# Second layer of a two-layer graph network: one tile in every fourth block by TensorE products instead of a gather

## The chip, the cores and the metric

The kernel runs on one core of one Trainium2 chip. Its measure is the device time of one execution in microseconds (us). The engines are PE (TensorE: matmuls; PEld is its weight load), DVE (VectorE), ACT (ScalarE), POOL (GpSimd) and SP (SyncE). Each works through its own instructions in order, and they meet at semaphores. Here POOL issues only gathers in the main part, and SP issues plain DMAs.

## The reference, cut to what matters

There are 6250 nodes with 128 features and 200,000 edges (src, dst), sorted by dst. Two layers follow each other, each on a normalized x: a graph attention layer, then a tensor product layer. What the change touches is the second one:

```python
h = relu(layernorm(x))
s, v = h[:, :32] @ W_up_s / sqrt(32), einsum(h[:, 32:], W_up_v) / sqrt(32)
w0, w1, w2, w3 = split(silu(silu(edge_feats @ A1 + b1) @ A2 + b2) @ A3, 4)   # per edge
ss, vs = s[src], v[src]                                                     # the gather
m = [ss * y_s * w0, (vs . y_v) / sqrt(3) * w3, ss * y_v * w1, vs * y_s * w2]  # 256 per edge
message = segment_sum(m, dst) / 10
x = x + [message_s @ W_out_s, message_v @ W_out_v] / 8
```

Because the edges are sorted by dst, the sum over an edge's target is a matmul with a one-hot matrix of local target numbers.

## The kernel before, in words

An edge tile is 128 edges; a block is 16 tiles (KB), except the last with 11. There are 98 blocks (NB), 1563 tiles, and 50 node tiles (NX). The first layer leaves a table t1 in DRAM: 128 float32 values (s and v) per node. The second layer starts at L1617. It works in units of four tiles (list us), four units to a block.

The order of the work on PE, DVE, ACT and SP is the order in which the Python program calls the operations (manual_schedule with in_order). POOL holds only the gathers, also in the program's order.

For each unit i of the loop at L1795 the order is:
- at the first unit of a block: take_rows(b + 2), the gathers of the block two further on; filled, which copies a row tile into place (ACT, L1096); edge_rows(b + 2), two loads by SP (L1631, L1633); every second block a load of x (L1709).
- rows_until, which advances SP's copies of single rows (below).
- network(b + 1): one of four steps of the edge network of the next block (PE L1650 or L1654, ACT L1652 or L1657).
- tensor_weights(i + 1): the weights of the next unit (PE L1667) and their scaling by y_s (ACT L1671).
- messages(i): seven DVE operations, L1687 to L1696, which read the gathered rows z and write mj.
- one_hot(i + 1) (DVE L1101), then the end of a block (finish, L1114) and node1 (L1711), and sums1(i) (PE L1704), which adds the unit's messages into PSUM.

A gather fetches the 128 rows of one edge tile, one indirect DMA issued by POOL (L834). A block's rows land in a buffer g of the pool fz, which has five of them (L976); block 0 has z_first. A buffer is free once the block's last messages have read it.

Two ways around the gather exist. In every third block (by_row, L1057) the last tile's 128 rows are copied one by one by SP (L1082), after offsets are loaded into registers 32 at a time (L1078). rows_until (L1089) keeps this three blocks ahead, so the first unit of a layer starts with 35 steps of 4 rows. In the first layer, in the blocks of dense (L1127), tile KD = 14 is made of matmuls: the table is held in SBUF as three bf16 parts that add up to its float32 values (t0s, split at L1167), a one-hot matrix picks the rows (L1198, L1211), and since the 50 node tiles are folded into 17 steps of up to three tiles, DVE picks the right one of three results (L1217, L1219).

The first 24 tiles of the second layer are gathered early, from a copy t1z of the table in which the last three node tiles are zero. late_ends and late_rows (L1744, L1758) add the missing rows by matmuls in the first units.

PSUM has eight banks; in the second layer p_h, p_w and p_u have two each, p_n one, and held one (iota, and yp, a copy of y_v in three places by turns).

Of the kernel before, what the change touches and what calls it, by code (L numbers as in the profile page):

```python
# [965 lines left out]
def even_edges(tc, v):  # L966
# [7 lines left out]
    with ExitStack() as ctx:  # L974
# [123 lines left out]
        def one_hot(t, m, iota=iota):  # L1098

            s = s_pool.tile([P, 4, P], F32, name="s")  # L1100
# [21 lines left out]

        NR = -(-NX // 3)
        KD = KB - 2
        dense = {b for b in range(6, NB - 4) if b % 2}  # L1127


        in_order = {mybir.EngineType.PE, mybir.EngineType.DVE, mybir.EngineType.Activation,  # L1130
                    mybir.EngineType.SP}
        with tc.manual_schedule(engines=in_order), \
# [10 lines left out]
            nc.scalar.copy(iota_p, iota)  # L1143
            nc.scalar.mul(node_p, jp[:, 0:1], -1.0)


            ND = NB - 1
            key = l0d.tile([P, ND], F32, name="key")
            nc.vector.tensor_scalar(key, src_col[:, KD : ND * KB : KB], float(W0), None, op0=OP.add)
            part = l0d.tile([P, ND, 3], F32, name="part")  # L1150
            nc.vector.tensor_single_scalar(part[:, :, 1], key, float(NR * P), op=OP.is_ge)
            nc.vector.tensor_single_scalar(part[:, :, 2], key, float(2 * NR * P), op=OP.is_ge)
            nc.vector.tensor_add(part[:, :, 0], part[:, :, 1], part[:, :, 2])
            nc.vector.scalar_tensor_tensor(key, part[:, :, 0], -float(NR * P), key,
                                           op0=OP.mult, op1=OP.add)
            nc.vector.tensor_sub(part[:, :, 1], part[:, :, 1], part[:, :, 2])
            nc.vector.tensor_single_scalar(part[:, :, 0], part[:, :, 0], 0.0, op=OP.is_equal)

            order = sorted(range(NR), key=lambda k: (k > 0, 2 * NR + k < NX, k))
            half = (NR + 1) // 2  # L1160
            place = l0d.tile([P, NR], F32, name="place")
            for j, k in enumerate(order):
                nc.vector.tensor_scalar(place[:, j : j + 1], jp[:, 0:1], -1.0, float(P * k),
                                        op0=OP.mult, op1=OP.add)
            t0s = l0d.tile([P, 3, NX, ZW], BF, name="t0s")

            def split(i, n):  # L1167

                zr = l0.tile([P, 2, ZW], F32, name="zr")[:, :n]
                if i == 0:  # L1170
                    nc.vector.memset(zr[:W0, 0, :], 0.0)
                    nc.sync.dma_start(zr[W0:, 0, :], t0[: P - W0, :])
                    rest = t0[P - W0 : n * P - W0]
                    nc.sync.dma_start(zr[:, 1:], rest.rearrange("(j p) f -> p j f", p=P))
                else:
                    rest = t0[i * P - W0 : (i + n) * P - W0]
                    nc.sync.dma_start(zr, rest.rearrange("(j p) f -> p j f", p=P))
                r = l0.tile([P, 2, ZW], F32, name="zr2", bufs=1)[:, :n]
                nc.scalar.copy(t0s[:, 0, i : i + n, :], zr)
                nc.vector.tensor_sub(r, zr, t0s[:, 0, i : i + n, :])  # L1180
                nc.scalar.copy(t0s[:, 1, i : i + n, :], r)
                nc.vector.tensor_sub(t0s[:, 2, i : i + n, :], r, t0s[:, 1, i : i + n, :])

            def spread(c):

# [284 lines left out]
            for g in range(NG - 3):  # L1470
# [73 lines left out]
                if to:  # L1544
                    rows_of(n2, 6, half - 6)
                for i in range(g * 14, min(g * 14 + 14, NX), 2):
                    split(i, min(2, NX - i))
                if g == NG - 4:
                    for q in range(4):
                        ends_of(c1, q)  # L1550
# [66 lines left out]
        with tc.manual_schedule(engines=in_order), \  # L1617
                tc.tile_pool(name="l1", bufs=3) as l1, \
                tc.tile_pool(name="l1n", bufs=2) as l1n, \
                tc.tile_pool(name="l1_ps", bufs=2, space=PSUM) as l1_ps:  # L1620

            a3p = l1.tile([P, 2, P], F32, name="fa3p", bufs=1)
# [12 lines left out]
            def network(b, step):  # L1635

                c = blk[b]
                q0, second = step // 2 * 4, step % 2
                if 2 * q0 >= KT[b]:
                    return  # L1640
                if step == 0:
                    c["h2"] = []
                if step == 3 or 2 * q0 + 8 >= KT[b] and second:
                    c["yp"] = held[:, P + b % 3 * KB * 3 : P + (b % 3 + 1) * KB * 3].rearrange(
                        "p (t i) -> p t i", i=3)
                    nc.scalar.copy(c["yp"], c["yb"][:, :, 1:4])  # L1646
                p_h = l1_ps.tile([P, 4, P], F32, name="p_h")
                if not second:
                    for q in range(4):
                        nc.tensor.matmul(p_h[:, q, :], a1p[:, q0 + q, :], c["ft"], start=True, stop=True)  # L1650
                    c["h1"] = l1.tile([P, 4, P], F32, name="h1")
                    nc.scalar.activation(c["h1"], p_h, AF.Silu, bias=b1)  # L1652
                else:
                    nc.tensor.matmul(p_h.rearrange("p q e -> p (q e)"), a2p,  # L1654
                                     c["h1"].rearrange("p q e -> p (q e)"), start=True, stop=True)
# [54 lines left out]

            def node1(i, agg):  # L1711
                x_i = x_of[i][:, 0, :]
                p_n = l1_ps.tile([P, 4, P], F32, name="p_n", bufs=1)
                for q in range(2):
                    nc.tensor.transpose(p_n[:, q, :], agg[:, q * P : (q + 1) * P], ident)
                m_t = l1n.tile([P, 2, P], F32, name="m_t")
                nc.scalar.copy(m_t, p_n[:, :2])  # L1717
                for q in range(2):
                    nc.tensor.matmul(p_n[:, 2, :], m_t[:, q, :], wout[:, q, :], start=q == 0, stop=q == 1)  # L1719
                nc.vector.scalar_tensor_tensor(x_i, p_n[:, 2, :], POST, x_i, op0=OP.mult, op1=OP.add)  # L1720
                return i

            def node_out1(i):
# [34 lines left out]
            def late_rows(t):  # L1758
                if t < NE:
                    z, k0, oh = blk[t // KB]["z"], t % KB, late_ends.of.pop(t)  # L1760
                    p_n = l1_ps.tile([P, 4, P], F32, name="p_n", bufs=1)
                    for k in range(4):
                        for j in range(NL):
                            nc.tensor.matmul(p_n[:, k, :], oh[:, j, k, :], sv_late[:, j, :],
                                             start=j == 0, stop=j == NL - 1)
                    z = z[:, k0 : k0 + 4, :P]
                    nc.vector.tensor_add(z, z, p_n)

            blk = [{} for _ in range(NB)]
            us = [{"b": b, "k0": k0, "m": min(4, KT[b] - k0)}  # L1770
# [3 lines left out]
            def take_rows(b):  # L1774
                if b in early:
                    blk[b]["z"] = gather(early[b], t1, range(max(b * KB, NE), b * KB + KB), P,
                                         max(NE - b * KB, 0))
                elif b < NB:
                    blk[b]["z"] = gathered(t1, range(b * KB, b * KB + KT[b] - (b in by_row)), P)

            rows, rows_until.n, late, x_of = rows_by_row(1, t1, P), 0, [], {}
            for b in range(2):
# [5 lines left out]
            for step in range(4):  # L1788
                network(0, step)
            tensor_weights(us[0])  # L1790
            us[0]["s"] = one_hot(0, us[0]["m"], iota_p)
            ready, done = [], []
            carry = agg = None
            ends = None
            for i, u in enumerate(us):  # L1795
                b, k0, m = u["b"], u["k0"], u["m"]
                if k0 == 0:
# [11 lines left out]
                if i + 1 < NU:  # L1809
                    tensor_weights(us[i + 1])  # L1810
                late_ends(4 * (i + 2))
                messages(u)
                late_rows(4 * (i + 1))
                if i + 1 < NU:
                    n = us[i + 1]
                    n["s"] = one_hot(n["b"] * KB + n["k0"], n["m"], iota_p)
# [18 lines left out]
            p_n = l1_ps.tile([P, 4, P], F32, name="p_n", bufs=1)  # L1835
# [152 lines left out]
```

## Time and profile before

| | |
|---|---|
| Time, median of 3 runs | 3953.19 us (3948.89 to 3955.46) |
| The profiled execution's own time | 6235.86 us |
| Its span, first to last instruction | 6234.0 us |
| Mean granted PE clock in it | 0.728 |
| Busy: PE, PEld, DVE, ACT, POOL | 3133, 2416, 2621, 1191, 2872 us |
| Gathers of the main part (L834) | 2980, 945 ns each |
| Single-row copies by SP (L1082) | 7936 |
| Second layer in it, from the first gather of t1 | 3052.77 us to the end |

A line of a group shows the source line, the engine, the operation, output and inputs, how often it occurs, then busy time and mean duration in ns, then the idle time of the engine just before and what ended it. A line of the timeline shows start and duration in us, then the same names; in brackets the idle time before it and what ended that. "issue" stands for idle time in which the engine waited for nothing that the profile shows. The profiled execution is much longer than the timed ones, so times of the page and those of the runs are not compared directly.

### The profile page before, as it was taken

The page shows a single profiled execution, that of the slowest core. Times are in us where ns is not written, and L with a number is a line of the kernel's source. Part 1 is how long each engine was busy: PE and PEld are TensorE (multiplying, and loading weights), DVE is VectorE, ACT ScalarE, POOL GpSimd, SP SyncE. Part 2 cuts the span into 40 slices and gives each one's busy share as a digit, 9 for nine tenths or more (in the row PEclk, how much of TensorE's full clock was granted, in tenths as well). Part 3 has the DMA queues.
Part 4 walks back from the last instruction along what each step waited for, and adds up shares of the span by engine and source line. Part 5 has one row for each costly group of instructions (what it writes and reads, how often), then busy time and mean ns, then how long its engine had stood idle before and what let it go on. Part 6 is the DMA issues. An engine that isn't in the chain of part 4 may idle for free. (4 is left out here: it accounts for less than half of the span.)

```text
span 6234.0 us, 64789 instructions
## 1 busy us (share of the span) xinstructions
PE 3133.4 (50%) x15554; PEld 2416.2 (39%) x15554; DVE 2620.8 (42%) x6094; ACT 1190.7 (19%) x3272; POOL 2872.4 (46%) x3052
## 2 busy tenths in 40 slices
PE   2145454444444444444355555555555555555557
PEld 1133333333333333333344444444444444444445
DVE  3244444444444444444333444444443444443446
ACT  1111111111111111111122222222222222222223
POOL 6144444444454454455534444444444444444442
PEclk6567677667667766777577777777777777777778
DMA  5122222222222222222111111111111111111111
GB/s 141 41 61 58 63 59 60 61 58 58 62 60 58 58 63 59 57 61 66 54 26 39 38 39 37 39 39 39 39 36 38 39 40 39 37 37 37 40 39 26
DMA packets 230951, 311.54 MB, mean 50 GB/s; under 512 B 83328, under 2 KB 168928, under 8 KB 230560
## 3 DMA queue, kind: packets, MB, share of 16 engines
q0 software_dynamic: 96640, 204.21, 13.8%
q1 hardware_dynamic: 133632, 103.03, 5.6%
q8 instruction: 125, 2.05, 0.1%
q14 instruction: 266, 2.18, 0.1%
q10 hardware_dynamic: 288, 0.07, 0.0%
HBM read 289.79 MB, written 16.95 MB: 49 GB/s over the span
## 5 line engine op out<-in xcount | busy, mean ns | idle before, releaser
L834 POOL DMA_INDIRECT g<-ft,fsrc x2980 | 2816.1, 945 | 3241.3 <-issue 1119.4
L1704 PE MATMUL p_u<-mj,s 128*128 128x256 f32 x3126 | 930.0, 450 | 680.8 <-DVE mj L1696 572.6
L1704 PEld LDWEIGHTS p_u<-mj,s 128*128 128x128 f32 x3126 | 682.6, 226 | 865.7 <-DVE mj L1696 623.4
L1251 DVE TENSOR_TENSOR d<-er_d,p_i 128x512 bf16<-128x512 bf16 x391 | 264.5, 677 | 863.1 <-DMA er_d<-fends_d 787.6
L1101 DVE TENSOR_TENSOR s<-p_i,fdloc 128x512 f32<-128x512 f32 x782 | 533.0, 682 | 197.2 <-PE p_i L1187 135.6
L1689 DVE TENSOR_TENSOR p_w<-g,p_w 128x128 f32<-128x128 f32 x387 | 112.9, 292 | 1178.2 <-ACT p_w L1671 1024.2
L1211 PE MATMUL p_x<-t0s,fz_first 128*128 128x408 bf16 (+1 forms) x2244 | 559.6, 409 | 29.9 <-issue 29.6
L1333 PE MATMUL p_u<-g,s 128*128 128x136 f32 x3062 | 537.4, 348 | 7.2 <-issue 4.4
L1671 ACT ACTIVATE p_w<-p_w,yb 128x64 f32<-128x64 f32 x1563 | 449.7, 288 | 461.2 <-remote 238.0
L1333 PEld LDWEIGHTS p_u<-g,s 128*128 128x128 f32 x3062 | 514.8, 255 | 7.7 <-issue 7.5
L1302 PE MATMUL pe<-mx,fshift 128*128 128x1 f32 (+1 forms) x194 | 55.8, 357 | 741.9 <-issue 514.7
L1667 PE MATMUL p_w<-fa3p,h 128*128 128x256 f32 x1564 | 422.7, 395 | 0.0
L1667 PEld LDWEIGHTS p_w<-fa3p,h 128*128 128x128 f32 x1564 | 303.3, 204 | 143.5 <-issue 106.0
L1657 ACT ACTIVATE h<-p_h,fb 128x512 f32<-128x512 f32 x196 | 134.7, 687 | 1141.9 <-remote 796.3
L1211 PEld LDWEIGHTS <-fz_first 128*128 128x128 bf16 x2244 | 250.8, 115 | 244.8 <-issue 152.5
L1719 PE MATMUL p_n<-fwout,m_t 128*128 128x128 f32 x192 | 57.6, 454 | 563.6 <-ACT m_t L1717 563.6
L1302 PEld LDWEIGHTS pe<-mx,fshift 128*128 128x128 f32 (+1 forms) x194 | 47.6, 305 | 749.9 <-issue 520.1
L1654 PE MATMUL p_h<-h,fa2p 128*128 128x512 f32 x392 | 248.0, 720 | 168.5 <-ACT h L1652 145.5
L1261 PEld LDWEIGHTS <-d 128*128 128x128 bf16 x1563 | 105.9, 122 | 513.0 <-DVE d L1251 378.0
L1687 DVE TENSOR_TENSOR vy<-g,p_i 128x384 f32<-128x384 f32 x387 | 211.3, 546 | 179.6 <-ACT p_i L1646 178.1
L1652 ACT ACTIVATE h<-p_h,fb 128x512 f32<-128x512 f32 x196 | 134.3, 685 | 726.8 <-PE p_h L1650 373.8
L1719 PEld LDWEIGHTS p_n<-fwout,m_t 128*128 128x128 f32 x192 | 43.7, 316 | 576.6 <-ACT m_t L1717 576.6
(220 smaller groups left out, 3667.6 us busy)
## 6 DMA issues: line engine op xcount, KB each, us to landing
r<-ft SPq DMA_DIRECT2D x3968, 0.5 KB
r<-ft SPq DMA_DIRECT2D x3968, 0.5 KB
er_d<-fends_d SPq DMA_DIRECT2D x98, 512.0 KB
g<-ft,fsrc POOLq DMA_INDIRECT x2980
ft<-in_e_f_dram SPq DMA_DIRECT2D x98, 64.0 KB
zr<-ft SPq DMA_DIRECT2D x24, 136.0 KB
yb<-in_e_y_dram SPq DMA_DIRECT2D x98, 32.0 KB
x<-in_e_xp_dram SPq DMA_DIRECT2D x48, 64.0 KB
```

Of the source, the lines that this page charges most:

```text
L834: nc.gpsimd.indirect_dma_start(out=to[:, k, :width], out_offset=None, in_=table, in_offset=bass.IndirectOffsetOnAxis(ap=src_col[:, t : t + ...
L1101: nc.vector.tensor_tensor(s[:, :m], iota[:, None, :].to_broadcast([P, m, P]), dloc[:, t : t + m].unsqueeze(2).to_broadcast([P, m, P]), OP. ...
L1211: nc.tensor.matmul(c["p_x"][:, :m, :], c["oh", k // half][:, k % half, :], t0s[:, s, i::NR, :], start=k == 0 and s == 0, stop=k == NR - 1 ...
L1251: nc.vector.tensor_tensor(d[:, :m], ends_row.tiles[c["b"]][:, k0 : k0 + m], node_p.unsqueeze(2).to_broadcast([P, m, P]), OP.is_equal)
L1333: nc.tensor.matmul(c["p_u"][:, :ZW], c["s"][k // 4][:, k % 4, :], c["z"][:, k, :], start=c["o"] + k == 0, stop=c["o"] + k == KT[c["b"]] - 1)
L1652: nc.scalar.activation(c["h1"], p_h, AF.Silu, bias=b1)
L1654: nc.tensor.matmul(p_h.rearrange("p q e -> p (q e)"), a2p, c["h1"].rearrange("p q e -> p (q e)"), start=True, stop=True)
L1657: nc.scalar.activation(h2, p_h, AF.Silu, bias=b2)
L1667: nc.tensor.matmul(w[:, k : k + n].rearrange("p k a u -> p (k a u)"), c["h2"][q // 4][:, q % 4, :], a3p[:, :n].rearrange("p k f -> p (k f) ...
L1671: nc.scalar.activation(w[:, k, ::2, :], w[:, k, ::2, :], AF.Copy, scale=c["yb"][:, k0 + k, 0:1])
L1687: nc.vector.tensor_mul(vy, v_n, y_p)
L1704: nc.tensor.matmul(blk[b]["p_u"][:, :MW], u["s"][:, k, :], u["mj"][:, k, :], start=k0 + k == 0, stop=k0 + k == KT[b] - 1)
```

## The change

The second layer gets what the first has. In blocks 8, 12, ..., 92 (dense1, 22 of 98) tile 14 is no longer gathered. Its rows are products of a one-hot matrix with t1, held in SBUF as three bf16 parts (t1s, 38,400 bytes per partition). The table is read back from DRAM by SP in 25 pieces of two node tiles (node_tiles) and split by two ACT casts and two DVE subtractions a piece (in_three), one piece in each of the first 25 units, ahead of that unit's messages. The products of a dense block are spread over the last two units of the block before and its own first three (dense_step). node1's p_n moves into the bank of held, beside iota and yp; the bank that it leaves, p_x, serves late_rows and the new products. yp now alternates between two places, not three. The pool of s buffers in the second layer has 5, not 16. Functions for the first layer's table are shared by both (ends_in_ranges, node_tiles, in_three).

```diff
-        s_pool = ctx.enter_context(tc.tile_pool(name="fs", bufs=16))
+        s_pool = of_l0.enter_context(tc.tile_pool(name="fs", bufs=16))
...
+        dense1 = set(range(8, NB - 4, 4))
...
+        def node_tiles(pool, table, width, i, n, bufs=2):
+            zr = pool.tile([P, 2, width], F32, name="zr", bufs=bufs)[:, :n]
...
+                nc.sync.dma_start(zr, rest.rearrange("(j p) f -> p j f", p=P))
+            return zr
+
+        def in_three(pool, zr, width, t_s, i, n):
+            r = pool.tile([P, 2, width], F32, name="zr2", bufs=1)[:, :n]
+            nc.scalar.copy(t_s[:, 0, i : i + n, :], zr)
+            nc.vector.tensor_sub(r, zr, t_s[:, 0, i : i + n, :])
+            nc.scalar.copy(t_s[:, 1, i : i + n, :], r)
+            nc.vector.tensor_sub(t_s[:, 2, i : i + n, :], r, t_s[:, 1, i : i + n, :])
...
-                    c["yp"] = held[:, P + b % 3 * KB * 3 : P + (b % 3 + 1) * KB * 3].rearrange(
+                    c["yp"] = held[:, P + b % 2 * KB * 3 : P + (b % 2 + 1) * KB * 3].rearrange(
...
-                p_n = l1_ps.tile([P, 4, P], F32, name="p_n", bufs=1)
...
-            iota_p = held[:, :P]
+            iota_p, p_n = held[:, :P], held[:, 2 * P :].rearrange("p (j f) -> p j f", f=P)
...
+            key, part, place_r = ends_in_ranges(l1n)
+            t1s = l1d.tile([P, 3, NX, P], BF, name="t1s")
+
+            def dense_ends(b):
+                p_x = blk[b]["p_x"] = l1_ps.tile([P, 4, P], F32, name="p_x", bufs=1)
+                nc.tensor.matmul(p_x[:, 3, :], key[:, b : b + 1].to_broadcast([P, P]), ident,
+                                 start=True, stop=True)
+                oh = blk[b]["oh"] = l1d.tile([P, NR, P], BF, name="ohs")
+                for k, n in ((0, half), (half, NR - half)):
+                    nc.vector.tensor_tensor(
+                        oh[:, k : k + n], p_x[:, 3:4, :].to_broadcast([P, n, P]),
+                        place_r[:, k : k + n].unsqueeze(2).to_broadcast([P, n, P]), OP.is_equal)
+
+            def dense_rows(b, k0, n):
+                c = blk[b]
+                for k in range(k0, min(k0 + n, NR)):
+                    i = order[k]
+                    m = len(range(i, NX, NR))
+                    for s in range(3):
+                        nc.tensor.matmul(c["p_x"][:, :m, :], c["oh"][:, k, :], t1s[:, s, i::NR, :],
+                                         start=k == 0 and s == 0, stop=k == NR - 1 and s == 2)
...
+            def dense_step(b, q):
+                if b + 1 in dense1:
+                    if q == 1:
+                        dense_ends(b + 1)
+                    elif q > 1:
+                        dense_rows(b + 1, (q - 2) * 4, 4)
+                if b in dense1:
+                    dense_rows(b, 8 + 3 * q, 3)
+                    if q == 2:
+                        dense_taken(b)
...
+            zrs = [node_tiles(l1d, t1, P, j, 2, 3) for j in (0, 2)]
             for i, u in enumerate(us):
...
                 late_ends(4 * (i + 2))
+                if 2 * i + 4 < NX:
+                    zrs.append(node_tiles(l1d, t1, P, 2 * i + 4, min(2, NX - 2 * i - 4), 3))
+                if zrs:
+                    in_three(l1d, zrs.pop(0), P, t1s, 2 * i, min(2, NX - 2 * i))
                 messages(u)
+                dense_step(b, k0 // 4)
                 late_rows(4 * (i + 1))
```

More of the change, by code (lines that the diff above doesn't have):

```diff
@@ L1096, in filled, with one_hot @@
                 nc.scalar.copy(z[:, KB - 1, :width], rows_by_row.tiles.pop((layer, b)))
-        def one_hot(t, m, iota=iota):
-            s = s_pool.tile([P, 4, P], F32, name="s")
+        def one_hot(t, m, iota, pool=s_pool):
+            s = pool.tile([P, 4, P], F32, name="s")
             nc.vector.tensor_tensor(s[:, :m], iota[:, None, :].to_broadcast([P, m, P]),
@@ L1126, in even_edges, with ends_in_ranges @@
         KD = KB - 2
+        order = sorted(range(NR), key=lambda k: (k > 0, 2 * NR + k < NX, k))
+        half = (NR + 1) // 2
         dense = {b for b in range(6, NB - 4) if b % 2}
+        dense1 = set(range(8, NB - 4, 4))
+        def ends_in_ranges(pool):
+            ND = NB - 1
+            key = pool.tile([P, ND], F32, name="key")
+            nc.vector.tensor_scalar(key, src_col[:, KD : ND * KB : KB], float(W0), None, op0=OP.add)
+            part = pool.tile([P, ND, 3], F32, name="part")
+            nc.vector.tensor_single_scalar(part[:, :, 1], key, float(NR * P), op=OP.is_ge)
+            nc.vector.tensor_single_scalar(part[:, :, 2], key, float(2 * NR * P), op=OP.is_ge)
+            nc.vector.tensor_add(part[:, :, 0], part[:, :, 1], part[:, :, 2])
+            nc.vector.scalar_tensor_tensor(key, part[:, :, 0], -float(NR * P), key,
+                                           op0=OP.mult, op1=OP.add)
+            nc.vector.tensor_sub(part[:, :, 1], part[:, :, 1], part[:, :, 2])
+            nc.vector.tensor_single_scalar(part[:, :, 0], part[:, :, 0], 0.0, op=OP.is_equal)
+            place = pool.tile([P, NR], F32, name="place_r")
+            for j, k in enumerate(order):
+                nc.vector.tensor_scalar(place[:, j : j + 1], jp[:, 0:1], -1.0, float(P * k),
+                                        op0=OP.mult, op1=OP.add)
+            return key, part, place
@@ new lines, in node_tiles @@
+        def node_tiles(pool, table, width, i, n, bufs=2):
+            zr = pool.tile([P, 2, width], F32, name="zr", bufs=bufs)[:, :n]
+            if i == 0:
+                nc.vector.memset(zr[:W0, 0, :], 0.0)
+                nc.sync.dma_start(zr[W0:, 0, :], table[: P - W0, :])
+                rest = table[P - W0 : n * P - W0]
+                nc.sync.dma_start(zr[:, 1:], rest.rearrange("(j p) f -> p j f", p=P))
+            else:
+                rest = table[i * P - W0 : (i + n) * P - W0]
+                nc.sync.dma_start(zr, rest.rearrange("(j p) f -> p j f", p=P))
+            return zr
@@ L1144, in even_edges @@
             nc.scalar.mul(node_p, jp[:, 0:1], -1.0)
[L1147 to L1164, printed above, removed]
-            t0s = l0d.tile([P, 3, NX, ZW], BF, name="t0s")
[L1167 to L1182, printed above, removed]
+            key, part, place = ends_in_ranges(l0d)
+            t0s = l0d.tile([P, 3, NX, ZW], BF, name="t0s")
             def spread(c):
@@ L1546, in even_edges @@
                 for i in range(g * 14, min(g * 14 + 14, NX), 2):
-                    split(i, min(2, NX - i))
+                    n = min(2, NX - i)
+                    in_three(l0, node_tiles(l0, t0, ZW, i, n), ZW, t0s, i, n)
                 if g == NG - 4:
@@ L1619, in even_edges @@
                 tc.tile_pool(name="l1n", bufs=2) as l1n, \
+                tc.tile_pool(name="l1s", bufs=5) as l1s, \
+                tc.tile_pool(name="l1d", bufs=1) as l1d, \
                 tc.tile_pool(name="l1_ps", bufs=2, space=PSUM) as l1_ps:
@@ L1716, in node1 @@
                 m_t = l1n.tile([P, 2, P], F32, name="m_t")
-                nc.scalar.copy(m_t, p_n[:, :2])
+                nc.scalar.copy(m_t, p_n)
                 for q in range(2):
-                    nc.tensor.matmul(p_n[:, 2, :], m_t[:, q, :], wout[:, q, :], start=q == 0, stop=q == 1)
-                nc.vector.scalar_tensor_tensor(x_i, p_n[:, 2, :], POST, x_i, op0=OP.mult, op1=OP.add)
+                    nc.tensor.matmul(p_n[:, 0, :], m_t[:, q, :], wout[:, q, :], start=q == 0, stop=q == 1)
+                nc.vector.scalar_tensor_tensor(x_i, p_n[:, 0, :], POST, x_i, op0=OP.mult, op1=OP.add)
                 return i
@@ L1760, in late_rows @@
                     z, k0, oh = blk[t // KB]["z"], t % KB, late_ends.of.pop(t)
-                    p_n = l1_ps.tile([P, 4, P], F32, name="p_n", bufs=1)
+                    p_l = l1_ps.tile([P, 4, P], F32, name="p_x", bufs=1)
                     for k in range(4):
                         for j in range(NL):
-                            nc.tensor.matmul(p_n[:, k, :], oh[:, j, k, :], sv_late[:, j, :],
+                            nc.tensor.matmul(p_l[:, k, :], oh[:, j, k, :], sv_late[:, j, :],
@@ L1765, in late_rows @@
                                              start=j == 0, stop=j == NL - 1)
                     z = z[:, k0 : k0 + 4, :P]
-                    nc.vector.tensor_add(z, z, p_n)
+                    nc.vector.tensor_add(z, z, p_l)
+            key, part, place_r = ends_in_ranges(l1n)
[9 more added lines that the diff above has]
+                        place_r[:, k : k + n].unsqueeze(2).to_broadcast([P, n, P]), OP.is_equal)
@@ new lines, in dense_rows, with dense_taken @@
+            def dense_rows(b, k0, n):
[6 more added lines that the diff above has]
+                                         start=k == 0 and s == 0, stop=k == NR - 1 and s == 2)
+            def dense_taken(b):
+                c = blk[b]
+                z = c["z"][:, KD, :P]
+                nc.vector.tensor_scalar(z, c["p_x"][:, 0, :], part[:, b, 0:1], None, op0=OP.mult)
+                for r in (1, 2):
+                    nc.vector.scalar_tensor_tensor(z, c["p_x"][:, r, :], part[:, b, r : r + 1], z,
+                                                   op0=OP.mult, op1=OP.add)
@@ L1778, in take_rows @@
                 elif b < NB:
-                    blk[b]["z"] = gathered(t1, range(b * KB, b * KB + KT[b] - (b in by_row)), P)
+                    blk[b]["z"] = gathered(t1, [k for k in range(b * KB, b * KB + KT[b])
+                                                if not (b in by_row and k % KB == KB - 1)
+                                                and not (b in dense1 and k % KB == KD)], P)
             rows, rows_until.n, late, x_of = rows_by_row(1, t1, P), 0, [], {}
@@ L1790, in even_edges @@
             tensor_weights(us[0])
-            us[0]["s"] = one_hot(0, us[0]["m"], iota_p)
+            us[0]["s"] = one_hot(0, us[0]["m"], iota_p, l1s)
             ready, done = [], []
@@ L1815, in even_edges @@
                     n = us[i + 1]
-                    n["s"] = one_hot(n["b"] * KB + n["k0"], n["m"], iota_p)
+                    n["s"] = one_hot(n["b"] * KB + n["k0"], n["m"], iota_p, l1s)
                 if ends is not None:
@@ L1834, in even_edges @@
             first = (NX - 2) * P - W0
-            p_n = l1_ps.tile([P, 4, P], F32, name="p_n", bufs=1)
+            p_n = l1_ps.tile([P, 4, P], F32, name="p_x", bufs=1)
             for j in range(2):
```

## The prediction

> **What bounds the kernel now.** I read the page first: its span, then the rows of GpSimd (POOL), which issues the gathers.
>
> ```profile
> span 6234.0 us, 64789 instructions
> PE 3133.4 (50%) x15554; PEld 2416.2 (39%) x15554; DVE 2620.8 (42%) x6094; ACT 1190.7 (19%) x3272; POOL 2872.4 (46%) x3052
> ...
> L834 POOL DMA_INDIRECT g<-ft,fsrc x2980 | 2816.1, 945 | 3241.3 <-issue 1119.4
> ```
>
> Nothing is above 50%, and the profiled execution (6235.9 us) is 58% longer than the median of the three timed runs (3953.2 us). So the page's shares can't be taken as they stand. The timeline of the DMA queue of SP says why: first a stretch near 5533 us, then one 10 us later.
>
> ```profile
> 5533.09 6.40 SPq L1082 DMA_DIRECT2D r<-ft  x20
> ```
>
> ```profile
> 5543.74 7.07 SPq L1082 DMA_DIRECT2D r<-ft  x6
> ```
>
> A row copy costs 0.32 us in the first and 1.18 us in the second. In stretches of the second kind PE, ACT and DVE stand still as well, while POOL goes on. I take them to be the profiler's own. Outside them the kernel runs at its natural pace; all durations below are from there. Now POOL's timeline at the start of the second layer:
>
> ```profile
> 3052.77 0.94 POOL L834 DMA_INDIRECT g<-ft,fsrc  x1 [24.91 <-issue]
> 3054.01 0.95 POOL L834 DMA_INDIRECT g<-ft,fsrc  x1 [0.31 <-issue]
> ...
> 3140.14 0.94 POOL L834 DMA_INDIRECT g<-ft,fsrc  x1 [0.30 <-issue]
> 3210.88 0.94 POOL L834 DMA_INDIRECT g<-ft,fsrc  x1 [69.79 <-DVE mj L1696]
> ```
>
> Gathers start every 1.249 us. After 71 of them (8 left of block 1, 16, 15, 16, 16) POOL needs the buffer of block 1, which the last message product (L1696) of that block frees: its lead over the computation is 71 gathers, 88.7 us, and no more.
>
> Sum for the whole: first gather at 42.5 us, 2980+16+16+8 = 3020 gathers x 1.249 = 3772 us, two waits at the border of the layers (6.7 and 24.9 us): 3846 us. That leaves 107 us of the median for a wait at the start and the tail: the timed kernel fits POOL issuing gathers nearly without a break, where the profiled one can't (POOL 46% busy). Per block of the second layer POOL needs 1532/98 = 15.6 gathers, 19.5 us. The computation is faster: four units (quarters of a block) in a row start their sums (L1704) at 6083.16, 6087.40, 6090.99 and 6094.64 us, 3.8 us each, about 15.5 us a block. SP needs 42.7 rows x 0.32, 1.33 loads of offsets x 2.13 and some three copies x 0.45, 18 us.
>
> **What the Trainium skill says.** "TensorE: Matmul & The Clock Gate", section "Architectural detail: the array is 16× 32×32, not 1× 128×128", calls ACT and DVE strict FIFOs: what stands ahead in program order must be done. The trace agrees; see the 110.63 us below. The same page, section "What's actually happening", has PE's clock halved after an idle window of about 3.4 us. The trace shows half clock even after an idle 1.96 us: eight sums took 1.99 us in one unit and 3.67 us in the next. "SBUF — State Buffer", section "SBUF: two separate sides", says that DVE and GpSimd share a port pair as an exclusive lock, which a DVE operation with two SBUF inputs can hold against a GpSimd operation that reads SBUF. Here gathers took 938 to 1504 ns, median 944; the case is rare.
>
> **The change, part by part.** I set zero at the second layer's first gather from t1 (3052.77).
>
> *Gathers.* Blocks 8, 12, ..., 92 lose one each: 22 x 1.249 = 27.5 us off POOL's queue.
>
> *Products that take their place.* The first layer shows them: 51 matmuls per block, nine of 128x408 in 1.72 us, so 0.16 us each at 384 columns, 8.4 us; the two comparisons (L1198) 1.34 and 1.22 us; three operations of 0.36 us. For four blocks PE needs 4 x 15.5 + 8.4 + 0.4 = 70.8 us, DVE some 4 x 13.4 + 3.6 = 57 us, POOL (4 x 15.6 - 1) x 1.249 = 76.7 us. Both are hidden by the gathers; without that cover they would cost 8.8 us per such block on PE.
>
> *Joined banks, fewer s buffers.* node1's transposes move into the bank of iota; yp alternates between two places. The readers of the place before are a block old, and at most two s tiles live at once. Nothing, or below 1 us per two blocks.
>
> *The comparisons' constants.* 17 operations of 150 ns (L1163's row) and some eight more join DVE's queue at the border, partly between steps that t1's last rows wait for: 3 us.
>
> *The table in three parts.* This is the expensive part. In each of the first 25 units two ACT casts and two DVE subtractions stand ahead of messages(u), cast and subtraction in turn. The first layer shows such a chain, and what ACT does when the table's rows are late:
>
> ```profile
> 235.45 0.42 ACT L1179 CAST t0s<-zr 128x272 bf16<-128x272 f32 x1 [110.63 <-DMA zr<-ft]
> 235.90 0.44 DVE L1180 TENSOR_TENSOR zr<-zr,t0s 128x272 f32<-128x272 f32 x1 [66.41 <-ACT t0s L1179]
> ...
> 236.37 0.42 ACT L1181 CAST t0s<-zr 128x272 bf16<-128x272 f32 x1 [0.51 <-DVE zr L1180]
> ...
> 236.82 0.44 DVE L1182 TENSOR_TENSOR t0s<-zr,t0s 128x272 bf16<-128x272 f32 x1 [0.48 <-ACT t0s L1181]
> ```
>
> The chain takes 1.8 us. Two things make it cost more.
>
> First, SP. The table's third piece is issued in unit 0 behind that unit's rows: 35 steps of 4, 140 rows. Start of rows 2.4 us (profile) + 1.3 for the three earlier copies; 140 x 0.32 = 44.8; four more loads of offsets, 8.5; issue and landing 2.6 (236.37 to 238.59 in the first layer). It is there at 59.7 us, and unit 2 waits for it. With the chain and the messages (2.5 us) unit 2's messages end at 64 us. Before, nothing in units 2 to 7 waited for SP.
>
> Second, the loop closes. Before, messages(i) needed weights that were scaled one unit earlier, so DVE ran beside PE. Now ACT's first cast in unit i stands behind the scaling of unit i+1, that behind PE's products of unit i, those behind sums1(i-1), which wait for messages(i-1). The timeline of one unit without such casts has the pieces:
>
> ```profile
> 6058.21 0.54 DVE L1696 TENSOR_TENSOR mj<-g,p_w 128x384 f32<-128x384 f32 x1
> ...
> 6058.80 1.99 PE L1704 MATMUL p_u<-mj,s 128*128 128x256 f32 x8
> ...
> 6060.63 1.02 PE L1654 MATMUL p_h<-h,fa2p 128*128 128x512 f32 x2
> ...
> 6061.49 1.03 PE L1667 MATMUL p_w<-fa3p,h 128*128 128x256 f32 x4
> ...
> 6062.08 1.25 ACT L1671 ACTIVATE p_w<-p_w,yb 128x64 f32<-128x64 f32 x4 [2.17 <-PE p_h L1654]
> ```
>
> From the end of the messages (6058.75) to the end of the scaling (6063.33) 4.6 us, the chain 1.8, the messages 2.5: 8.9 us a unit with PE at full clock. PE idles some 5.4 us of that, so its clock will often be halved, which costs the eight sums 1.7 us: 10.6 us. I take 10.1, against 4.9 us that POOL needs for four gathers.
>
> So messages of unit 3 end at 75 us (late_ends, about 1 us, is still in the chain), of unit 23 at 75 + 20 x 10.1 = 277, of unit 24 at 287, of unit 27 at 299 (three units of 4.0, free again). POOL, once its 71 gathers are out at 89 us, waits for every block: block 10 starts at 277 (block 5's buffer), block 11 at 299 (block 6's, and block 10's gathers end at 297). Before, block 11 starts after 71 + 15 + 16 + 16 + 15 + 16 = 149 gathers, at 186 us. POOL is late by 113 us; after that it isn't stopped again. SP's queue is held back too, as each further piece waits for a buffer that the casts free, but afterwards it needs 18 us a block against POOL's 19.
>
> The sum: 113 (stall) - 21 x 1.249 (block 8's gather is saved inside the stall) + 3 = 90 us. 3953 + 90 = **4043 us**.
>
> **Bounds.** With PE always warm (8.9 us, first wait the same) unit 27 ends at 273: +64, 4017. Rows at a third less than 0.32 us, if the profiler's marks weigh on them: 15 us less, 4002. Always half clock (10.6): +101, 4054; with subtractions that delay gathers (50 x 0.44 us at most, most of them within the stall) 4075. So the likeliest case alone spans 4002 to 4075.
>
> **Rivals.**
> - *The lead covers it.* If a unit took 5.9 us or less (75 + 21 x 5.9 + 12 = 211 = 186 + 26 - 1), POOL's delay would not exceed the saving; with no delay the time is 3953 - 27.5 = 3926. For it: the lead of 71 gathers, and the engines' busy times, which alone come to under 5 us a unit. Against: ACT's and DVE's program order.
> - *Half covered.* The rows come early and the chain overlaps partly: a unit of 7 us ends at 3977.
> - *PE binds later.* If a block took PE over 17 us while it follows POOL (half clock), the products would not be hidden; at 18.5 us four blocks need 82.8 against 76.7, and 22 times 6.1 is 134 us more, about 4180. Against: the sums' spacing, and no long gaps once units follow each other every 4.9 us.
> - *The change doesn't do what it says*: 22 gathers fewer must stand in POOL's rows; nothing speaks against it.
>
> **How the numbers follow.** Likeliest 0.80; lead covers 0.09; half covered 0.06; PE binds 0.05. From 3985 to 4082 leaves out the covered case, part of the half-covered one, and PE binding. About 0.2% is what a measurement of this kernel can tell from no change. Faster 0.10, same 0.02, slower 0.88.
>
> **What would show it.** In the changed profile: POOL's 71 gathers, then a wait for message products before each of blocks 6 to 11; ACT waiting for zr some 60 us (more where the profiler slows SP); in units 3 to 24 the casts behind the scaling and the sums a full loop apart, about 9 to 11 us; 2958 gathers in L834's first row; later PE no busier than POOL. I am wrong if messages in those units come every 5 to 6 us outside the slowed stretches, or if POOL isn't stopped there.

## The result, and the profile after

The changed kernel takes 4083.03 us (median of 4 runs, 4080.18 to 4085.91), the kernel before 3951.32 us (median of 4, 3948.89 to 3955.46): a ratio of 1.0331, 95% interval 1.0318 to 1.0344. It is 132 us slower, where the prediction said 90 us, and lies just above the predicted range. One thing has to be known of the times below: on three of the chips every kernel, the one before too, took about 1.6 times as long, because in stretches PE, DVE, ACT and SP stand still there; each run is compared with the kernel before on its own chip, and sizes are read from chips without such stretches.

The page of the changed kernel has its span (its own time is 4082.87 us, so this execution is like the timed ones), busy times and gathers:

```profile
span 4081.1 us, 67346 instructions
PE 2950.3 (72%) x16720; PEld 2298.7 (56%) x16720; DVE 2722.3 (67%) x6279; ACT 1233.1 (30%) x3322; POOL 2862.2 (70%) x3030
...
L834 POOL DMA_INDIRECT g<-ft,fsrc x2958 | 2805.8, 949 | 1162.6 <-issue 910.2
```

2958 gathers instead of 2980: the change does what it says. Each takes 0.95 us, but in this profile they start 1.252 us apart (median), so a POOL without a break shows as 76% busy, no more. In the page's 40 slices it is so in nearly all of the second layer, and at 20% just after the middle. POOL's timeline at that place, the start of the second layer, first its 71st and 72nd gather, then the first of block 10:

```profile
2139.56 0.95 POOL L834 DMA_INDIRECT g<-ft,fsrc  x1 [0.30 <-issue]
2175.30 0.94 POOL L834 DMA_INDIRECT g<-ft,fsrc  x1 [34.79 <-DVE mj L1708]
```

```profile
2363.11 0.94 POOL L834 DMA_INDIRECT g<-ft,fsrc  x1 [28.07 <-DVE mj L1708]
```

After 71 gathers, counted from the layer's first one (2051.45 us), POOL waits 35, 29, 26, 29, 28 and 7 us, once before each of blocks 6 to 11. The trace puts four of these waits down to message products (L1708, which was L1696), the third to nothing that it shows and the last to ACT; but each ends 0.3 to 0.8 us after the last message product of the block whose buffer is needed. To see what they cost, take the start of the 230th gather after the layer's first, less 230 x 1.25 us: it is late by 155 us. There is one more wait, of 1.9 us, before the 179th gather; from the 180th on none is over 0.32 us. So nearly all of the loss comes from the first 25 units, in which the table is built. One of these units, from the end of its predecessor's messages to its own, in the timeline:

```profile
2210.03 0.55 DVE L1708 TENSOR_TENSOR mj<-g,p_w 128x384 f32<-128x384 f32 x1
...
2210.64 3.78 PE L1716 MATMUL p_u<-mj,s 128*128 128x256 f32 x8 [5.51 <-DVE mj L1708]
...
2214.21 1.91 PE L1666 MATMUL p_h<-h,fa2p 128*128 128x512 f32 x2
...
2215.92 1.45 PE L1679 MATMUL p_w<-fa3p,h 128*128 128x256 f32 x4
...
2217.41 1.26 ACT L1683 ACTIVATE p_w<-p_w,yb 128x64 f32<-128x64 f32 x4 [0.56 <-PE p_w L1679]
2218.59 0.40 ACT L1168 CAST t1s<-zr 128x256 bf16<-128x256 f32 x1
2219.02 0.43 DVE L1169 TENSOR_TENSOR zr<-zr,t1s 128x256 f32<-128x256 f32 x1 [7.83 <-ACT t1s L1168]
...
2219.92 0.42 DVE L1171 TENSOR_TENSOR t1s<-zr,t1s 128x256 bf16<-128x256 f32 x1 [0.47 <-ACT t1s L1170]
...
2222.28 0.55 DVE L1708 TENSOR_TENSOR mj<-g,p_w 128x384 f32<-128x384 f32 x1
```

Read it downwards: sums, network step, weights, scaling, cast, subtraction, messages, one behind the other, and then the sums of the next unit. That is the predicted loop, and it takes 12.25 us here. The products on PE are all slower than in the unit that the prediction shows: from the first sum to the start of the scaling it is 6.8 us, where it was 3.3 us there. Units 3 to 24 come 11.62 us apart on average (prediction: 10.1).

### The profile page after: what moved, and what is told of

It is laid out like the page before. It is cut to its first block, busy times and chain, and to the rows that moved or that the text cites. A ratio compares the mean times of both kernels' runs of the same rounds, so it can differ in the third digit from the quotient of the medians.

```text
span 4081.1 us, 67346 instructions
## 1 busy us (share of the span) xinstructions
PE 2950.3 (72%) x16720; PEld 2298.7 (56%) x16720; DVE 2722.3 (67%) x6279; ACT 1233.1 (30%) x3322; POOL 2862.2 (70%) x3030
## 5 line engine op out<-in xcount | busy, mean ns | idle before, releaser
L1716 PE MATMUL p_u<-mj,s 128*128 128x256 f32 x3126 | 805.9, 403 | 228.9 <-DVE mj L1708 227.8
L1716 PEld LDWEIGHTS p_u<-mj,s 128*128 128x128 f32 x3126 | 603.4, 200 | 374.2 <-DVE mj L1708 291.5
L1342 PE MATMUL p_u<-g,s 128*128 128x136 f32 x3062 | 492.7, 329 | 0.4 <-DVE g L1337 0.4
L1220 PE MATMUL p_x<-t0s,fz_first 128*128 128x408 bf16 (+1 forms) x2244 | 474.0, 365 | 0.0
L1342 PEld LDWEIGHTS p_u<-g,s 128*128 128x128 f32 x3062 | 470.7, 236 | 0.5 <-DVE g L1337 0.4
L1337 DVE TENSOR_TENSOR g<-g,pe 128x1024 f32<-128x1024 f32 x193 | 234.6, 1216 | 4.9 <-ACT g L1328 4.7
L1703 DVE TENSOR_REDUCE vd<-vy 128x128 f32<-128x384 f32 x391 | 230.0, 588 | 0.0
L1662 PEld LDWEIGHTS p_h<-ft,fa1p 128*128 128x128 f32 x1568 | 211.8, 196 | 17.2 <-issue 4.2
L1662 PE MATMUL p_h<-ft,fa1p 128*128 128x128 f32 x1568 | 212.0, 279 | 4.2 <-DMA ft<-in_e_f_dram 4.2
L1704 DVE TENSOR_TENSOR mj<-p_w,yb 128x384 f32<-128x384 f32 x391 | 214.9, 550 | 0.0
```

The costliest lines, as they stand in the source:

```text
L1220: nc.tensor.matmul(c["p_x"][:, :m, :], c["oh", k // half][:, k % half, :], t0s[:, s, i::NR, :], start=k == 0 and s == 0, stop=k == NR - 1 ...
L1337: nc.vector.tensor_mul(zh, zh, p_a[:, k0 : k0 + m].unsqueeze(3).to_broadcast([P, m, H, D]))
L1342: nc.tensor.matmul(c["p_u"][:, :ZW], c["s"][k // 4][:, k % 4, :], c["z"][:, k, :], start=c["o"] + k == 0, stop=c["o"] + k == KT[c["b"]] - 1)
L1703: nc.vector.tensor_reduce(vd, vy.rearrange("p t i u -> p t u i"), AX.X, OP.add)
L1704: nc.vector.tensor_mul(m_v1, sw.unsqueeze(2).to_broadcast([P, m, 3, MU]), y_v)
L1716: nc.tensor.matmul(blk[b]["p_u"][:, :MW], u["s"][:, k, :], u["mj"][:, k, :], start=k0 + k == 0, stop=k0 + k == KT[b] - 1)
```

## Experiments

The spacing below is the mean distance of the ends of messages from unit 3 to unit 24; "POOL late" is read at the 230th gather as above.

| Run | Time | Kernel before, same chip | Ratio, 95% interval | Spacing | POOL late |
|---|---|---|---|---|---|
| e6 changed kernel again | 4078.29 | 3950.83 | 1.0325 (1.0308 to 1.0342) | 11.47 | 152 |
| e7 five filler products | 4035.06 | 3950.83 | 1.0218 (1.0201 to 1.0235) | 9.42 | 107 |
| e8 products only | 3922.36 | 3950.83 | 0.9928 (0.9912 to 0.9945) | 4.54 | 0 |
| e9 before, banks joined | 3950.26 | 3950.83 | 0.9999 (0.9990 to 1.0008) | 4.56 | 0 |
| e14 casts behind, five pieces first | 3930.86 | 3951.27 | 0.9952 (0.9935 to 0.9968) | 5.58 | 2 |
| e15 casts behind | 3939.19 | 3948.71 | 0.9970 (0.9959 to 0.9982) | 5.45 | 17 |
| e16 as e14, every third block | 3988.42 | 3948.71 | 1.0097 (1.0080 to 1.0114) | 5.73 | 6 |

### Casts behind the messages (e1, e1b, e10, e15, e14)

The theory under test is the closed loop: messages(i) wait for the casts of unit i, these for the scaling of unit i+1, and so for the sums of unit i-1. The same work a few lines further down opens it:

```diff
-                if zrs:
-                    in_three(l1d, zrs.pop(0), P, t1s, 2 * i, min(2, NX - 2 * i))
                 messages(u)
...
                     n["s"] = one_hot(n["b"] * KB + n["k0"], n["m"], iota_p, l1s)
+                if zrs:
+                    in_three(l1d, zrs.pop(0), P, t1s, 2 * i, min(2, NX - 2 * i))
```

> The same casts and subtractions, 25 pieces, but behind the messages and one_hot of their unit, so that messages(i) no longer wait for the scaling of unit i+1. Closed-loop theory: units 3 to 24 come 4.5 to 5.5 us apart instead of 11.6, and POOL's waits of 154 us after its 71 gathers shrink to under 20: 4083 - 139 to 154 us, so 3929 to 3944 us, below the kernel before by the 22 gathers less the border's 3 us. Rival one, the table's work or the products cost the time wherever they stand: 4083 us as in the changed kernel. Rival two, SP's late third piece is the cause: it is as late here, so again about 4083 us.

> The same kernel as in the run with casts behind the messages. There the kernel before took 6242 us, not 3951, because all engines but POOL have stretches in which they stand still; if this chip has none of them, the expectation is the old one. Closed-loop theory: units 3 to 24 come 4.5 to 5.5 us apart, POOL's waits after its 71 gathers stay under 20 us in all: 3929 to 3944 us, against 3951 before and 4083 with the casts ahead of the messages. Rival, the added work costs wherever it stands: 4083 us.

> The casts behind the messages and one_hot of their unit, for a chip where the kernel before takes 3951 us. Closed-loop theory: units 3 to 24 come 4.5 to 5.5 us apart, POOL's waits after its 71 gathers stay under 20 us in all; products alone gave 3922 us, so 3922 to 3942 us, below the kernel before. Rival, casts, subtractions and loads cost wherever they stand: near 4080 us. Where the kernel before takes 6235 us: 6344 as measured.

> The casts behind the messages, alone, once more. With five pieces ahead of the rows as well it was 3931 us and POOL 1.8 us late. Closed-loop theory: with the third piece late again (unit 2's messages end at 66 us) and units 4.5 to 5.6 us apart, unit 7's messages end at 90 to 95 us, 1 to 6 us after the 71 gathers: 3930 to 3937 us. Rival, the late piece carries more than the 22 us that I gave it: 3950 us or more. Where the kernel before takes some 6235 us: 6344 as measured.

Three of the four runs fell on chips with standstills: 6343.85 against 6242.50 us (1.017, 1.0145 to 1.0195), 6344.25 against 6232.81 (1.0172, 1.014 to 1.0204), 6417.25 against 6297.42 (1.0183, 1.0165 to 1.0202). There units come 7.5 to 8.1 us apart; in the kernel before on such a chip it is 7.4 us, and in the kernels there that cast ahead of the messages 12.2 to 12.8. The fourth run tells the rest: 3939.19 us, 139 us below the changed kernel on the same chip (e6) and below the kernel before. The rival that the work costs wherever it stands falls, and so does the one that SP's late piece is the cause, for that is as late here. The time is a little over the expected 3930 to 3937: POOL is 17 us late, since unit 3 now waits behind unit 2's late piece (its messages end at 68.3 us, unit 7's at 93.4) and units stay 5.45 us apart, slower than POOL's 4.9 us for four gathers, until the table is done. The 72nd gather waits 4.80 us, where it waited 34.79:

```profile
2145.16 0.94 POOL L834 DMA_INDIRECT g<-ft,fsrc  x1 [4.80 <-DVE mj L1708]
```

Hence the same with five pieces ahead of SP's rows, and six buffers for them:

```diff
-            zrs = [node_tiles(l1d, t1, P, j, 2, 3) for j in (0, 2)]
+            zrs = [node_tiles(l1d, t1, P, j, 2, 6) for j in (0, 2, 4, 6, 8)]
...
-                if 2 * i + 4 < NX:
-                    zrs.append(node_tiles(l1d, t1, P, 2 * i + 4, min(2, NX - 2 * i - 4), 3))
+                if 2 * i + 10 < NX:
+                    zrs.append(node_tiles(l1d, t1, P, 2 * i + 10, min(2, NX - 2 * i - 10), 6))
```

> Casts behind the messages, and five pieces of the table ahead of SP's 140 rows. Closed-loop theory: with neither the loop nor the late piece POOL isn't stopped after its 71 gathers, and the time is that of the products alone, 3922 us and up to 8 us for subtractions that hold up gathers: 3922 to 3930 us. Rival, casts and loads cost wherever they stand: near 4060 us. On chips where the kernel before takes some 6235 us: 6344 as with the casts moved alone, or up to 22 us less.

3930.86 us: faster than the kernel before and the changed one, and 1 us over the expected 3922 to 3930. The 72nd gather does not wait:

```profile
2141.26 1.18 POOL L834 DMA_INDIRECT g<-ft,fsrc  x1 [0.30 <-issue]
```

A unit in its timeline, from messages to messages:

```profile
2166.78 0.55 DVE L1708 TENSOR_TENSOR mj<-g,p_w 128x384 f32<-128x384 f32 x1
2166.85 1.25 ACT L1683 ACTIVATE p_w<-p_w,yb 128x64 f32<-128x64 f32 x4 [0.18 <-PE p_w L1679]
...
2167.38 1.99 PE L1716 MATMUL p_u<-mj,s 128*128 128x256 f32 x8 [0.56 <-DVE mj L1708]
2168.03 0.40 ACT L1168 CAST t1s<-zr 128x256 bf16<-128x256 f32 x1
...
2169.35 0.43 DVE L1171 TENSOR_TENSOR t1s<-zr,t1s 128x256 bf16<-128x256 f32 x1 [0.47 <-ACT t1s L1170]
...
2171.72 0.54 DVE L1708 TENSOR_TENSOR mj<-g,p_w 128x384 f32<-128x384 f32 x1
```

The scaling of the next unit runs beside the messages, the casts beside the sums, and this unit takes 4.94 us (5.58 on average). The eight sums take 1.99 us instead of 3.78, with PE idle for 0.56 us before them instead of 5.51.

### Half clock (e5, e7)

The spacing was 11.6 us and not 10.1. To see whether PE's clock is the missing part, PE gets matmuls in its gap, whose result is not read:

```diff
                 messages(u)
+                if 5 <= i < 25:
+                    p_f = l1_ps.tile([P, 4, P], F32, name="p_x", bufs=1)
+                    for k in range(9):
+                        nc.tensor.matmul(p_f[:, :, :], ident, a1p[:, :4, :], start=True, stop=True)
```

> In units 5 to 24 PE gets nine matmuls of 128x512 more, whose results nobody reads, between the weights of unit i+1 and the sums of unit i, where it idled 5.5 to 5.9 us. They take 4.6 us at full clock. If PE's half clock is the part of the loop that my sum lacked: units 5 to 24 come 9.3 to 9.8 us apart instead of 11.6, 20 x 2 us less stall, about 4043 us. If the clock stays low in spite of them (rival), they take 9 us, delay the sums by 3 to 4 us a unit and the time goes to about 4150 us.

They were sized wrongly: nine of them took 9.6 us in that trace, not 4.6 (each shows as two records), longer than the gap, so they held the sums up: 6455.58 against 6242.50 us (1.0344, 1.0313 to 1.0375), on a chip with standstills, spacing 12.8. That run separates nothing. With range(5):

> Five matmuls of 128x512 instead of nine between the weights and the sums in units 5 to 24. The nine took some 9.6 us, longer than the gap, and held the sums up by about 3.5 us; five take 4.3 us at full clock and end before the messages do. If the half clock is the part of the loop that my sum lacked: units 5 to 24 come about 2 us closer than in the changed kernel (9.5 instead of 11.7, or 10.4 where it has 12.4), and the time is 40 us below the changed kernel's. Rival, the missing part is a wait and no work of PE: the spacing stays within 0.5 us, and so does the time within 10 us.

4035.06 us, 43 us less than the changed kernel on the same chip, and 9.42 us apart instead of 11.47, though PE does more. The table of stretches, of the changed kernel and of this one (columns: stretch, its length, busy time and instructions of PE, PEld, DVE, ACT, POOL, then the granted clock, DMA share, GB/s):

```profile
2175.00:2374.00 199.00, 103.24 (x304) 76.65 (x304) 68.95 (x177) 47.23 (x131) 66.38 (x70) 0.74 0.14 37
```

```profile
2175.00:2330.00 155.00, 133.29 (x452) 78.19 (x450) 67.47 (x173) 45.25 (x127) 60.57 (x64) 1.00 0.17 45
```

The clock is 0.74 in the loop and 1.00 with the filler. And in the timeline of e7 the sums, after an idle 1.21 us, are at full speed:

```profile
2231.01 4.46 PE L1877 MATMUL p_x<-fa1p,fident 128*128 128x512 f32 x10
...
2236.68 1.99 PE L1716 MATMUL p_u<-mj,s 128*128 128x256 f32 x8 [1.21 <-DVE mj L1708]
...
2238.51 1.02 PE L1666 MATMUL p_h<-h,fa2p 128*128 128x512 f32 x2
```

So the half clock is worth some 2.1 us a unit.

### The table alone, the products alone (e2, e11, e8)

```diff
-        dense1 = set(range(8, NB - 4, 4))
+        dense1 = set()
```

> The table is built as in the changed kernel, but no block uses it: all 3020 gathers are back and there are no products. Closed-loop theory: the 154 us stall stays, and the 21 gathers outside it come back: 4083 + 21 to 22 x 1.25 = 4109 us. Rival, the products or their PE time are what costs: back to about 3955 us. Half of each would show a value between.

> The table is built as in the changed kernel, ahead of the messages, and not used. Closed-loop theory: the changed kernel's 4078 to 4083 us and the gathers on top that it saved outside the stall, 22 x 1.25 at most: 4105 to 4110 us. Rival, the products take part in the loss: below 4080 us. Where the kernel before takes 6235 us: 6360 as measured.

Both fell on chips with standstills: 6360.20 against 6242.50 us (1.0198, 1.0173 to 1.0223) and 6418.88 against 6297.42 (1.0195, 1.0178 to 1.0212), spacing 12.4 us. So the table alone, with no product in the kernel, brings the loop. What it costs can't be read here, because on the chip of e2 the kernel with the casts moved (e1) lost 101 us too, against 118; on a chip without standstills it was not measured. The other half, products without table:

```diff
-            zrs = [node_tiles(l1d, t1, P, j, 2, 3) for j in (0, 2)]
...
-                if 2 * i + 4 < NX:
-                    zrs.append(node_tiles(l1d, t1, P, 2 * i + 4, min(2, NX - 2 * i - 4), 3))
-                if zrs:
-                    in_three(l1d, zrs.pop(0), P, t1s, 2 * i, min(2, NX - 2 * i))
                 messages(u)
+                if 2 * i < NX:
+                    nc.vector.memset(t1s[:, :, 2 * i : min(2 * i + 2, NX), :], 0.5)
```

> Products in the 22 blocks and no gathers for them, but the table is not read and split: DVE fills t1s with a constant piece by piece behind the messages, so these 22 tiles get wrong rows. That leaves out the table's loads, casts and subtractions, and with them the loop. If the products are hidden by the gathers: 22 x 1.249 us less than the kernel before and 3 us for the constants, 3927 us where that takes 3951. If products bind PE (rival): 3951 - 27 + 22 x up to 8.8, so up to 4118 us. On chips where the kernel before takes 6235 us no engine works without breaks, and more instructions may cost time by themselves: 6235 to 6345 us there.

3922.36 us, 28.5 us less than before (22 x 1.249 = 27.5). Its table holds a constant, so it leaves out the loads, casts and subtractions, and the products are the same work. They are hidden whole. The 72nd gather comes on time:

```profile
2138.79 0.94 POOL L834 DMA_INDIRECT g<-ft,fsrc  x1 [0.30 <-DVE mj L1707]
```

### The late third piece (e4, e12)

The edit of the second diff alone, casts ahead of the messages.

> Five pieces of the table are loaded ahead of SP's 140 rows instead of two, with six buffers; casts stay ahead of the messages. Closed-loop theory: ACT's wait of 23 us for the third piece in unit 2 goes, units 3 to 24 stay 11.6 us apart, and POOL's stall shrinks by about 22 us: 4061 us. Rival, SP's lateness sets the stall: most of 154 us goes, about 3935 us.

> Five pieces of the table ahead of SP's 140 rows, casts ahead of the messages. Closed-loop theory: unit 2 no longer waits 23 us for the third piece, units 3 to 24 stay 11.6 us apart: 22 us less, 4058 us. Rival, SP's lateness sets the stall: about 3935 us. Where the kernel before takes 6235 us: 6428 as measured.

Both on chips with standstills: 6428.15 against 6242.50 us (1.0301, 1.0274 to 1.0329) and 6497.98 against 6297.42 (1.0324, 1.0307 to 1.0341). The loop stays (spacing 12.2 and 12.3 us), so SP's lateness does not close it. The 22 us can't be read from these times; the wait behind them stands in the trace of the changed kernel. There the third piece ends ACT's wait at 62.3 us of the layer (unit 2's messages at 66.5):

```profile
2113.73 0.41 ACT L1168 CAST t1s<-zr 128x256 bf16<-128x256 f32 x1 [23.11 <-DMA zr<-ft]
```

With the casts behind, loading five pieces first took POOL's delay from 17 to 2 us (e15, e14). What it saves with the casts ahead was not measured on such a chip.

### Changed kernel again, banks joined (e6, e9)

> The changed kernel itself, beside the others. Where the kernel before takes 3951 us: 4083. On chips where the kernel before takes some 6235 us: the kernel with the casts behind the messages took 6344 there, and a stall longer by about 104 us (82 as with five pieces first, and 22 for the late third piece) gives 6448 us. Closed-loop theory: units 3 to 24 come about 12.4 us apart (11.6 in the other kind), against 7.6 with the casts behind the messages. Rival, the products cost the time: no difference to the kernel with the casts behind the messages, 6344 us.

4078.29 us: as in the result. e9 is the kernel before with `p_n` in the bank of `held`, `yp` at `b % 2`, `late_rows` in `p_x`, and `l1s` with five buffers for s:

> The kernel before with only the joined PSUM banks (node1's p_n beside iota and yp, yp in two places, late_rows in p_x) and the pool of five s buffers. My step says nothing or below 1 us per two blocks: equal to the kernel before within 0.3%. Rival, a reader of yp or of p_n now waits for the other user of the bank: up to 1 us x 49, 1.2% longer.

3950.26 against 3950.83 us: nothing, as the step said.

### Every third block (e13, e16)

```diff
-        dense1 = set(range(8, NB - 4, 4))
+        dense1 = set(range(8, NB - 4, 3))
```

> Casts behind the messages, and products in every third block from 8 (29 blocks) instead of every fourth (22). Three blocks ask PE for 3 x 15.8 + 8.8 = 56.2 us and POOL for (46.8 - 1) x 1.249 = 57.2 us. If PE keeps that margin: 7 x 1.25 = 9 us less than the kernel with every fourth. If waits of PE eat it (rival: PE binds): equal to it or up to 20 us longer.

6478.08 us on a chip with standstills, 61 more than e10, its base there. Then with e14 as the base:

> Casts behind the messages, five pieces ahead of the rows, and products in every third block from 8 (29 blocks) instead of every fourth (22). PE is busy 91% of the time in the second layer with 22 such blocks; three blocks ask it for 3 x 15.8 + 8.8 = 56.2 us and POOL for 57.2 us. If that margin holds: 7 x 1.25 = 9 us less than the 3931 us with every fourth, 3922 us. Rival, PE binds: 3931 us or up to 20 us more. Where the kernel before takes some 6235 us: about 60 us more than with every fourth, as measured.

3988.42 us, 58 more than e14 (which ran on another chip; the kernel before differs by 3 us between the two). The rival won, and by more than the 20 us that it was given. The last gather of each kernel and its span show where, e14 first:

```profile
3909.88 0.95 POOL L834 DMA_INDIRECT g<-ft,fsrc  x1 [0.30 <-issue]
```

```profile
span 3925.0 us, 67328 instructions
```

```profile
3919.93 0.94 POOL L834 DMA_INDIRECT g<-ft,fsrc  x1 [0.30 <-issue]
```

```profile
span 3987.3 us, 68112 instructions
```

POOL ends only 10 us later; the tail behind it grew from 15 to 67 us. In e16 POOL is held up for 1 to 2 us every six blocks, which come 115.8 us apart (92 gathers, 114.9 us by themselves): the computation needs 57.9 us for three blocks, not 56.2, and POOL alone would need 57.5. PE is busy 92% from 2450 to 3250 us and waits for DVE and ACT in the rest, so it is its work with these waits that binds. The computation does not gain back what it falls behind while the table is built, and at the end that is the tail. In the changed kernel and in e14, where POOL takes 77 us for four blocks, it does.

## Why the prediction was wrong in size

The sign, the place and the mechanism were right: POOL as the bound, 71 gathers of lead, then a wait for messages before each block, the casts behind the scaling, no stop later. The sum holds with the measured stall: 155 us, less 22 x 1.249 = 27.5 (the 155 are reckoned in the changed kernel's own gathers, so all 22 count), is 128 us, and measured were 132; in e6 it is 152 less 27.5, 124, and measured were 127. What is left is of the size of the 3 us for constants, but also of gathers that start 1.252 instead of 1.249 us apart, so no run shows these 3 us. Step by step:

- **What bounds it.** Right: in e9, the kernel before but for the joined banks, no gather of the second layer is late. Wrong: I took the stretches with standstills to be the profiler's own. Profiled executions on other chips have next to none, and the runs on chips that have them take 1.6 times as long unprofiled too; as far as these series go, they go with the chip. One number of the check on the whole kernel has them in it, the wait of 24.9 us at the border of the layers (4.0 in e9), but none of the sum for the change.
- **Gathers, products, joined banks.** Right: e8 and e9. A block's products keep PE busy for 8.9 us (predicted 8.4: nine matmuls in 1.72 us are 0.18 us each at 384 columns by plain division, where the step took 0.16). With the 3 us for constants e8 would have gained 24.5 us; it gained 28.5, interval 22 to 35, which allows them and their absence.
- **SP's late piece.** Right: there at 62.3 us (59.7), unit 2's messages end at 66.5 (64).
- **The loop.** The failed step, in its size: "PE idles some 5.4 us of that, so its clock will often be halved, which costs the eight sums 1.7 us: 10.6 us. I take 10.1". PE does idle, 5.5 us. But half clock does not end with the sums, to which the prediction charged all of it. In the 20 units from the one at 2151.9 us on, the granted clock is back at full 3.1 to 6.9 us after PE's restart, 4.6 on average, so network step and weights are slow too. Half of 4.6 us, an estimate, is 2.3 us a unit, and e7 gives 2.1 back. The Trainium skill, "TensorE: Matmul & The Clock Gate", section "What's actually happening", has it: about 3.4 us of sustained work, in a window that runs freely, before the clock is full. This trace agrees, with the 3.1 to 6.9 us above, up to two such windows. I had used that section for the way into half clock and not for the way out. The rest is 0.5 us in the warm loop (9.4 in e7, where I had 8.9); which of its parts was short stays open.
- **The stall.** 20 units that are 1.5 us longer are 31 us; the first units add 4, units 24 to 27 another 4. So block 11's first gather starts 39 us later than predicted, at 338.5 us of the layer and not at 299. The other 3 of the 42 us between 113 and 155 are the short wait before the 179th gather and block 8's gather, which the 113 leave in. Subtractions were allowed to delay gathers by at most 22 us; only five gathers of the layer took over 0.97 us, 0.8 us more than usual in all. The bound "always half clock (10.6)" was none, for the same reason: with all of PE's 3.3 us doubled it would have been 12.2 a unit, an estimate, and the range would have held the time. That e6, at 4078 us, lies within the range is a matter of a few us at its edge; the predicted stall is 42 us too short all the same.
- **Rivals.** "Lead covers it" and "half covered" fail by the spacing. "PE binds later" did not happen, but it was near: at every third block the computation did bind (e16). The sign "later PE no busier than POOL" was badly put: with 22 such blocks PE is busy 94% and POOL 76% from 2450 to 3250 us, and still POOL is the bound, because its 1.25 us hold 0.95 us of busy time.

## What to carry to other kernels

Where a few operations are added to a software pipeline, look up what each waits for in its engine's own order: between scaling and messages they joined two stages into one loop, and a few lines lower they cost almost nothing. A loop that leaves PE idle 5.5 us a turn paid for the way back to full clock each turn, in more of its products than the first: 2.1 us of a possible 3.3, so for a bound price all of PE's work there at half speed. And a bound with a lead shows no wait for as long as the lead lasts; whether the followers keep pace is read from the tail behind the last gather.

## What the runs showed of the hardware

Matmuls whose result nobody reads made a kernel 43 us faster (e7), because they keep PE at full clock. A PE gap well under 3 us can be enough for half clock: in e8's second layer the granted clock fell to half 12 times, and the longest gap of PE in the 8 us before was 1.75 to 2.86 us.

And the same kernel before took 3949 to 3951 us on some chips and 6233 to 6297 on others. Two lines from the end of its profile, taken where it is slow, show what happens there: ACT is idle for 13.80 us, until something that the profile doesn't show, while POOL gathers on (until it lacks a buffer).

```profile
6040.82 0.94 POOL L834 DMA_INDIRECT g<-ft,fsrc  x1 [0.30 <-issue]
6044.53 0.69 ACT L1657 ACTIVATE h<-p_h,fb 128x512 f32<-128x512 f32 x1 [13.80 <-remote]
```

What stops PE, DVE, ACT and SP isn't known from these traces. There, hidden work isn't free: the kernel with the casts moved, faster than before elsewhere, is 1.7 to 1.8% slower on them (e1, e1b, e10).
